# Cross-attention over eight batches: query chunks 4 to 7 of batches 0 and 1 by seven products of sums, and the softmax of seven quads divided after the value products

## The chip, the core and the metric

The program runs on one core of a Trainium2 chip. The metric is the device time of one execution, in microseconds; the median of three executions stands for a kernel. The core has five engines that run their own instruction streams in order: TensorE (PE in the profile, with its weight loads as PEld), VectorE (DVE), ScalarE (ACT), GpSimd (POOL) and SyncE (SP), which only issues transfers here. They wait for each other by semaphores. All data are 32-bit floats.

## The reference

One layer of cross-attention: layer norm of x, a query projection, attention of 32 heads of 32 columns over 256 context rows (which are keys and values at once), an output projection, and the residual.

```python
x = (hidden - mu) * rsqrt(var + 1e-5) * ln_gamma + ln_beta      # (8, 256, 1024)
Q = split_heads(x @ Wq.T)                                       # 32 heads of 32
scores = einsum('bhsd,bhtd->bhst', Q, K) * 32 ** -0.5           # K = V = context, (8, 256, 1024)
probs = softmax(where(mask, scores, -inf))
attn = einsum('bhst,bhtd->bhsd', probs, V)
return hidden + attn.reshape(B, S, 1024) @ Wout.T
```

## The kernel before

Work is cut into 64 **quads**. Quad n is batch n // 8 and query chunk n % 8: 128 columns of Q, which are four heads (0 to 3). For a quad, PE makes eight score products (`scores`, tiles `sc_n_j`, one PSUM bank a head, and there are four such banks in all, so the scores of quad n+1 overwrite those of quad n). VectorE adds the mask and takes the row's extreme (`exps`, the rows named CUSTOM_DVE_ANT_0 in the profile and ISA in an order, two for each head), ScalarE takes the exponential and sums it (tile `den`), VectorE inverts the sum (`normalize`, RECIPROCAL to `rden`), GpSimd or ScalarE multiplies the 128x256 tiles `e` by it, VectorE transposes them in blocks (`blocks`, STREAM_TRANSPOSE to `pT`), four transfers of SyncE swap blocks between partitions, with ScalarE's copies `pc` between, and PE multiplies with the values (`values`, tiles `pv`, 64 products a quad written as 32 in each of two halves). ScalarE copies the result to `at` (`copy_at`), in which the columns of a head stand on partitions.

A **query chunk** is `make_q`: eight products of 128x128 weights `wq` with `xnT`, eight for each of eight chunks and each batch. Batches 2 to 7 already go in pairs with seven products of sums instead of eight (`sum_x`, `sum_wq`, `query_product`, `copy_product`): the sums of weights replace the weights in `wq` and `ring`. Batches 0 and 1 go chunk by chunk. Chunks 0 to 2 of batch 0 stand ahead of the loop over quads, the others are spread over n = 0 to 9. Batch 0 carries one more column (257): the product of the weights with beta, which is the bias that batch 1 and later add in `copy_q`. Batch 0 is scaled by gamma in `copy_x0`; later batches have gamma folded into the weights (`fold`, eight sums 128x1024 on GpSimd).

The output projection of batch b runs in the eight quads after it (`product_steps`, tiles `po`), also by seven products of sums (`sum_wo`, `sum_at`).

What sets the order: all calls are recorded (`Recorded`) and issued by a table written out by number (`ORDER`), which fixes the order on each engine. The semaphores follow from it.

Names that the change and the prediction touch: `copy_x0`, `copy_x1`, `make_q`, `copy_q`, `fold`, `exps`, `normalize`, `copy_at`, the tiles `gs`, `qlo`, `ring`, `wo` (sums of output weights, empty early on), and `rp` (four tiles of 128x512, for residual rows, unused until the residuals of batch 0 are loaded).

## Time and profile before

| | us |
|---|---|
| median of three runs (lowest, highest) | 562.45 (561.54, 562.81) |
| the profiled execution's own time | 562.03 |
| span of its profile, first to last instruction | 560.2 |
| busy: PE, DVE, ACT, POOL | 553.7, 461.4, 441.1, 402.9 |
| chain that ended last: share of PE | 96% |

The span is what the prediction works on; 1.8 us lie around it. A row of the groups reads: line, engine, operation, tile written and tiles read, shape, count, then busy time, the mean length of one, and the idle time of that engine just before, with what ended it. Every instruction has the same line number, 371, since one recording helper issues them all, so tiles and not lines tell them apart. PE's records: one 128x128x256 product of the program is two records in the trace, so that a chunk of eight products shows as x16.

### The profile page before, as it was taken

The numbers are of one execution on the slowest core, as the hardware profiler recorded it, in microseconds if no ns is written. First come the engines' busy times: TensorE is split into PE (matmuls) and PEld (weight loads), VectorE is DVE, ScalarE is ACT, GpSimd is POOL, SyncE is SP. The second block draws the span as 40 slices with busy tenths as digits, with TensorE's granted clock in tenths as the row PEclk, the third lists the DMA queues.
The fourth block names the chain that finished last, engine by engine and source line by source line (L and its number), as shares of the span: only waits on it lengthen the run. The fifth ranks groups of instructions, "written<-read, shape, count | busy, mean of one in ns | idle before, by whom it ended". The sixth has DMA issues, their size and how long they took to land.

```text
span 560.2 us, 18699 instructions
## 1 busy us (share of the span) xinstructions
PE 553.7 (99%) x6586; PEld 371.3 (66%) x6586; DVE 461.4 (82%) x1709; ACT 441.1 (79%) x1475; POOL 402.9 (72%) x633
## 2 busy tenths in 40 slices
PE   7999999999999999999999999999999999999997
PEld 6778786676666675667675677566666666645544
DVE  5899889988788999878989889876786888888725
ACT  3599999889886797879777779878879768989930
POOL 1479989999789856678969676478773778467581
PEclk9999999999999999999999999999999999999999
DMA  8977777867587676789666867878657476765342
GB/s 298 346 228 236 201 207 207 245 163 198 177 262 250 182 204 183 204 234 273 164 183 209 221 174 209 240 206 226 152 158 212 112 218 187 221 197 135 95 115 112
DMA packets 46477, 112.64 MB, mean 201 GB/s; under 512 B 9008, under 2 KB 9776, under 8 KB 46384
## 3 DMA queue, kind: packets, MB, share of 16 engines
q1 hardware_dynamic: 40384, 91.52, 57.5%
q0 software_dynamic: 5712, 19.93, 11.5%
q8 instruction: 52, 0.85, 0.7%
q14 instruction: 41, 0.34, 0.2%
q10 hardware_dynamic: 288, 0.01, 0.0%
HBM read 58.99 MB, written 12.58 MB: 128 GB/s over the span
## 4 chain that ended last, share of the span: by engine, by line
PE 96%; DMA 2%; DVE 1%; issue 0%; ACT 0%
PE pq_P L371 26%; PE po_S L371 20%; PE sc L371 12%; PE pv L371 11%; PE po_A L371 11%; PE pq L371 10%; PE po_end L371 3%; PE po_last L371 1%; DMA x<-in_x_dram 1%; DMA k<-in_kv_dram 1%; PE px L371 1%; DMA gam<-in_gamma_dram 1%; PE po_end_s L371 0%; DVE pT L371 0%; DVE mb L371 0%; DVE e L371 0%
## 5 line engine op out<-in xcount | busy, mean ns | idle before, releaser
L371 ACT ACTIVATE e<-e,mn 128x256 f32<-128x256 f32 x512 | 256.0, 502 | 61.0 <-DVE mn L371 56.8
L371 POOL TENSOR_SCALAR e<-e,rden 128x256 f32<-128x256 f32 x408 | 191.4, 480 | 113.9 <-DVE rden L371 107.0
L371 DVE STREAM_TRANSPOSE pT<-e 128x512 f32<-128x512 f32 x256 | 177.3, 701 | 33.2 <-POOL e L371 24.4
L371 DVE CUSTOM_DVE_ANT_0 e<-sc,mb 128x256 f32<-128x256 f32 x512 | 192.4, 411 | 8.6 <-PE sc L371 4.0
L371 PE MATMUL pq_P<-xnT,wq 128*128 128x256 f32 x544 | 133.2, 383 | 0.1
L371 PEld LDWEIGHTS pq_P<-xnT,wq 128*128 128x128 f32 x544 | 101.5, 190 | 44.9 <-issue 29.6
L371 ACT ACTIVATION_READ_ACCUMULATOR e<-e,mn 128x1 f32 x512 | 97.2, 190 | 0.0
L371 ACT COPY pc<-pT 128x512 f32<-128x512 f32 x128 | 76.2, 611 | 11.1 <-DVE pT L371 8.4
L371 PE MATMUL po_S<-wo,at 128*128 128x512 f32 x152 | 74.0, 598 | 0.0
L371 DVE RECIPROCAL rden<-den 128x2 f32<-128x2 f32 x256 | 36.5, 151 | 32.2 <-ACT e L371 31.4
L371 PE MATMUL pq<-xnT,wq 128*128 128x256 f32 (+3 forms) x272 | 60.0, 372 | 1.3 <-DVE xnT L371 0.8
L371 PE MATMUL po_A<-wo,at 128*128 128x512 f32 x128 | 60.2, 600 | 0.0
L371 PE MATMUL pv<-pT,v_all 64*32 64x128 f32 x3584 | 59.4, 273 | 0.0
L371 PEld LDWEIGHTS pv<-pT,v_all 64*32 64x32 f32 x3584 | 51.3, 105 | 11.3 <-issue 5.7
L371 PEld LDWEIGHTS pq<-xnT,wq 128*128 128x128 f32 x272 | 48.0, 190 | 10.2 <-issue 2.8
L371 ACT ACTIVATE e<-e,rden 128x256 f32<-128x256 f32 x104 | 49.6, 501 | 3.3 <-DVE rden L371 3.1
L371 PE MATMUL po_S<-wo,s 128*128 128x512 f32 x104 | 51.0, 600 | 0.0
L371 PE MATMUL sc<-k,qa 32*128 32x256 f32 x640 | 47.4, 401 | 0.0
L371 PEld LDWEIGHTS sc<-k,qa 32*128 32x128 f32 x640 | 30.0, 184 | 18.9 <-issue 10.6
L371 DVE DVE_READ_ACCUMULATOR2_ANT mn<- 128x1 f32 x512 | 42.5, 83 | 0.0
L371 PEld LDWEIGHTS po_S<-wo,at 128*128 128x128 f32 x152 | 28.1, 190 | 19.4 <-issue 16.4
L371 PEld LDWEIGHTS po_A<-wo,at 128*128 128x128 f32 x128 | 23.5, 190 | 24.5 <-issue 22.5
(97 smaller groups left out, 603.6 us busy)
## 6 DMA issues: line engine op xcount, KB each, us to landing
pT<-pT SPq DMA_DIRECT2D x128, 128.0 KB, 3.2
pT<-pc SPq DMA_DIRECT2D x128, 128.0 KB, 3.7
v_all<-in_kv_dram POOLq DMA_DIRECT2D x17, 512.0 KB, 5.0
k<-in_kv_dram SPq DMA_DIRECT2D x30, 256.0 KB, 3.8
r<-in_x_dram SPq DMA_DIRECT2D x26, 256.0 KB, 4.3
xnT<-xe SPq DMA_DIRECT2D x92, 64.0 KB, 3.5
out_dram<-r POOLq DMA_DIRECT2D x18, 256.0 KB, 3.5
wq<-in_wq_dram SPq DMA_DIRECT2D x8, 512.0 KB, 8.5
```

What stands on the lines that cost most here:

```text
L371: getattr(getattr(self.nc, other.get(i, engine)), name)(*a, **k)
```

## The change

Three things, and a new order table.

Chunks 4 to 7 of batches 0 and 1 (a 512-column half of Q, 512 rows in two batches) are made by seven products of sums, of eight 128x128x256 matmuls each (`head_product`), where `make_q` took eight such groups. Four sums of weights (`head_sum_w`, in two halves each, 128x512) go to parts of `wo` that are empty early on; four sums of inputs (`head_sum_x`, in two halves each) go to `ring`, into batch 0's `xnT` and to `wo`. The products' results are copied or added by `head_copy`. Chunks 0 to 3 are made as before.

So that sums of both batches fit together, gamma is applied to batch 1's rows too (`copy_x1`, now eight ScalarE instructions with scale and bias, 128x256, where four plain copies of 128x512 stood), the score's scale is applied to gamma and beta beforehand, and `copy_q` is a plain copy. `fold` of the weights comes later.

Quads 1 to 7 are no longer divided before the value products. Their 28 reciprocals on VectorE and 56 multiplications of 128x256 (40 on GpSimd, 16 on ScalarE) go. In their place `turn_dens` makes, for each quad, one reciprocal of the 128x8 sums, one block transpose of 128x32, a transfer to DRAM and one back that spreads it over the partitions (128x256, into tiles of `rp`), and `copy_at` is followed by one GpSimd product of 128x256.

```diff
+    def head_sum_w(to, o, engine=nc.gpsimd):
+        a, b = {"T1": ("B12", "B11"), "T2": ("B22", "T1"), "T3": ("T2", "B11"), "T4": ("B21", "T2")}[to]
+        engine.tensor_tensor(H_T[to][:, o], H_T[a][:, o], H_T[b][:, o], ALU.subtract)
+
+    def head_sum_x(to, part, engine=nc.gpsimd):
+        a, b, op = {
+            "S1": ("A21", "A22", ALU.add), "S2": ("S1", "A11", ALU.subtract),
+            "S4": ("A12", "S2", ALU.subtract), "S3": ("A22", "S2", ALU.subtract),
+        }[to]
+        to, a, b = (H_X[of]()[:, ts(part, 2), :S] for of in (to, a, b))
+        engine.tensor_tensor(to, a, b, op)
+
+    def head_product(name):
...
+        if begins:
+            h_po[0] = ps_q.tile([P, 512], F32, tag="pq", name=f"ph_{name}_0")
+            h_po[1] = ps_o.tile([P, 512], F32, tag="po", name=f"ph_{name}_1")
+        wide = x_.shape[2]
+        for o in range(2):
+            for c in range(NK):
+                nc.tensor.matmul(
+                    h_po[o][:, :wide], w[:, o, c], x_[:, c], start=begins and c == 0, stop=c == NK - 1,
+                    skip_group_check=True,
+                )
+
+    def head_copy(name, o):
+        po = h_po[o]
+        if name in ("P1", "P2", "P5"):
+            to = {"P1": h_u[:, o], "P2": qa[:, H + o], "P5": h_v[:, o]}[name]
+            nc.scalar.copy(to, po[:, : S + 1])
+        elif name == "P6":
+            nc.vector.tensor_tensor(h_u[:, o, :S], po[:, :S], h_u[:, o, :S], ALU.add)
+            nc.gpsimd.tensor_tensor(h_v[:, o], h_v[:, o], h_u[:, o], ALU.add)
+        elif name == "P3":
+            nc.vector.tensor_tensor(qa[:, H + 2 + o], po[:, : S + 1], h_v[:, o], ALU.add)
...
+    HEAD_Q = {1: ("P1",), 2: ("P2",), 3: ("P5",), 4: ("P6", "P3"), 8: ("P7", "P4")}
+    HEAD_W = {0: ("T1", "T2"), 1: ("T3", "T4")}
+    HEAD_X = {1: ("S1",), 2: ("S2",), 3: ("S4", "S3")}
...
+    def turn_dens(n):
+        away = dram.tile([K, NA * K], F32, tag=f"dens_{n}", name=f"dens_{n}")
+        nc.vector.reciprocal(dens_of[n][:, : 2 * NH], dens_of[n][:, : 2 * NH])
+        nc.vector.transpose(turned[n], dens_of[n])
+        nc.sync.dma_start(
+            away.rearrange("c (a k) -> a c k", a=NA),
+            turned[n],
+        )
+        nc.sync.dma_start(
+            factors[n],
+            away[: 2 * NH].rearrange("(j s) q -> j (s q)", j=NH).unsqueeze(1).to_broadcast([NH, HD, T]),
+        )
...
+            if n in DEFER:
+                if j == 1:
+                    turn_dens(n)
+                return
...
+        if NQ * b + NK * k + c in DEFER:
+            at = ats[b, k][:, c].rearrange("p s a k -> p (s a k)")
+            nc.gpsimd.tensor_tensor(at, at, factors[NQ * b + NK * k + c], ALU.mult)
...
- 'foldat': [1, 1, 3, 3, 4, 5, 6, 7],
+ 'foldat': [5, 6, 7, 8, 3, 3, 4, 4],
...
-0-38 40-41 39 44 42 47 43 49-50 45 54-59 61 60 62-75 79-81 77 84-86 93 76 78 83 87-90 94-95 91-92 96-109
+32-33 35 34 36-38 43 40 39 42 41 44 51 50 46 45 54-55 0-19 56 58 57 59-60 64 84-85 61-63 65-71 20-24 72-74
```

What the new table does is seen in the engines' rows. First PE, between the scores of quad 5 and those of quad 6. Before, after the value products of quad 1, it reads (`pq_n` is the n-th query chunk, 8 and up are batch 1's):

```order
L371 MATMUL pq_7_262<-xnT_0_132,wq_120 128x257 x3
L371 MATMUL pq_8_286<-xnT_1_180,wq_120 128x256 x3
L371 MATMUL pq_9_291<-xnT_1_180,wq_120 128x256 x6
L371 MATMUL pq_8_286<-xnT_1_180,wq_120 128x256 x3
L371 MATMUL sc_6_0_312<-k_6_268,qa_119 128x256
```

and now, from the last row of quad 5's scores on (`ph_P6_0` and `ph_P6_1` are the two halves of the product P6):

```order
L374 MATMUL ph_P6_0_266<-xnT_0_132,wo_126 128x256
L374 MATMUL ph_P6_1_267<-xnT_0_132,wo_126 128x256
L374 MATMUL ph_P6_0_266<-xnT_0_132,wo_126 128x256
L374 MATMUL ph_P6_1_267<-xnT_0_132,wo_126 128x256 x2
L374 MATMUL ph_P3_0_268<-xnT_0_132,wq_120 128x257
L374 MATMUL ph_P6_1_267<-xnT_0_132,wo_126 128x256
L374 MATMUL ph_P3_0_268<-xnT_0_132,wq_120 128x257
L374 MATMUL ph_P3_1_269<-xnT_0_132,wq_120 128x257
L374 MATMUL ph_P3_0_268<-xnT_0_132,wq_120 128x257 x2
L374 MATMUL ph_P3_1_269<-xnT_0_132,wq_120 128x257 x2
L374 MATMUL pq_8_288<-xnT_1_184,wq_120 128x256 x2
```

Products of sums of batch 0 stand where two chunks of batch 1 stood, and the first of batch 1 comes only at the end; one bank takes P6_0, P3_0 and then chunk 8.

Second, VectorE in the same place, where quad 5's mask-adds end and its transposes begin. Before:

```order
L371 ISA e_5_2_300,mn_5_2_301<-sc_5_2_289,mb_0_142 128x256
L371 ISA mn_5_2_301 128x1
L371 STREAM_TRANSPOSE xe_2_308<-x_2_214 128x32x32
L371 RECIPROCAL rden_5_1_307<-den_5_1_299 128x2
L371 STREAM_TRANSPOSE pT_5_292<-e_5_0_294 128x8x64
L371 ISA e_6_0_321,mn_6_0_322<-sc_6_0_312,mb_0_142 128x256
L371 ISA mn_6_0_322 128x1
L371 RECIPROCAL rden_5_3_310<-den_5_3_306 128x2
```

and now:

```order
L374 ISA e_5_3_278,mn_5_3_279<-sc_5_3_265,mb_0_146 128x256
L374 ISA mn_5_3_279 128x1
L374 RECIPROCAL qlo_121<-qlo_121 128x8
L374 STREAM_TRANSPOSE pT_5_270<-e_5_0_272 128x8x64
L374 TENSOR_TENSOR qa_119<-ph_P3_1_269,ring_105 128x257
L374 STREAM_TRANSPOSE pT_5_270<-e_5_1_274 128x8x64
L374 STREAM_TRANSPOSE pT_5_270<-e_5_2_276 128x8x64
L374 ISA e_6_1_295,mn_6_1_296<-sc_6_1_283,mb_0_146 128x256
```

The reciprocals of single heads are gone from between, one for a whole quad is there, and an addition out of PSUM (P3's second half) has come in.

Third, GpSimd from quad 0's last multiplication on. Before:

```order
L371 TENSOR_SCALAR e_0_3_161<-e_0_3_161,rden_0_3_174 128x256 x2
L371 TENSOR_SCALAR e_1_1_188<-e_1_1_188,rden_1_1_198 128x256 x2
L371 TENSOR_SCALAR e_1_0_185<-e_1_0_185,rden_1_0_194 128x256 x2
L371 TENSOR_SCALAR e_1_2_191<-e_1_2_191,rden_1_2_199 128x256 x2
L371 TENSOR_SCALAR e_1_3_195<-e_1_3_195,rden_1_3_200 128x256 x2
L371 TENSOR_TENSOR wq_120<-wq_120,gs_118 128x1024
```

and now (`wo<-wq` are the sums of weights, `ring<-xnT` and `xnT<-ring` the first sums of inputs, `x_2` the layer norm of batch 2):

```order
L374 TENSOR_SCALAR e_0_3_165<-e_0_3_165,rden_0_3_178 128x256 x2
L374 TENSOR_TENSOR wo_126<-wq_120 128x512
L374 TENSOR_TENSOR wo_126<-wq_120,wo_126 128x512 x2
L374 TENSOR_TENSOR wo_126<-wo_126,wq_120 128x512
L374 TENSOR_TENSOR wo_126<-wq_120 128x512
L374 TENSOR_TENSOR wo_126<-wq_120,wo_126 128x512 x2
L374 TENSOR_TENSOR wo_126<-wo_126,wq_120 128x512
L374 TENSOR_TENSOR rstd_2_235<-ve_2_0_237,mhalf_110 128x1
L374 TENSOR_TENSOR ring_105<-xnT_1_184 128x2x256 x2
L374 TENSOR_SCALAR x_2_211<-x_2_211,mv_2_234,rstd_2_235 128x1024
L374 TENSOR_TENSOR xnT_0_132<-ring_105,xnT_0_132 128x2x256
```

Eight sums of 128x512 and then sums of inputs stand where quads 1 and later were multiplied.

443 lines of the change are left out of this document (245 added, 198 removed).

## The prediction

> **What bounds the kernel now.** First the page: its busy line, PE's slices and the chain that ended last.
>
> ```profile
> span 560.2 us, 18699 instructions
> PE 553.7 (99%) x6586; PEld 371.3 (66%) x6586; DVE 461.4 (82%) x1709; ACT 441.1 (79%) x1475; POOL 402.9 (72%) x633
> PE   7999999999999999999999999999999999999997
> PE 96%; DMA 2%; DVE 1%; issue 0%; ACT 0%
> ```
>
> TensorE is busy in every slice but the first and the last, and 96% of the chain is its own work. A busy row can hide waits, so second the table of who waited for whom, PE alone, which is complete with these five rows:
>
> ```profile
> PE busy L371 <- POOL ring masks.py:199: 1.4, 1, 1.4
> PE pq L371 <- DVE xnT L371: 0.8, 1, 0.8
> PE pq L371 <- ACT xnT L371: 0.5, 1, 0.5
> PE px L371 <- DVE x L371: 0.4, 1, 0.4
> PE sc L371 <- issue: 0.3, 1, 0.3
> ```
>
> All 3.4 us of it lie in the first 13 us. Third, pieces of the chain in order of time (start, length, what, count), for the price of a piece of PE's work:
>
> ```profile
> 59.61 2.04 PE pv L371 x119
> 104.44 1.09 PE pv L371 x64
> 105.52 2.77 PE po_S L371 x6
> 115.83 2.58 PE po_S L371 x6
> 118.40 3.45 PE pq_P L371 x16
> ```
>
> A chunk of eight query products (x16) takes 3.45 us, 0.43 a product; an output product takes 0.86 (2.58 for three). The same three cost 0.2 more where a run of full-width products begins after scores or values (2.77). The values of two quads together take 2.04, of one 1.09. So after the head the time is the sum of PE's pieces, and what is taken off PE comes off the end, as long as nobody else becomes late.
>
> The Trainium skill's page "Perfetto Trace Analysis" (Identifying the Most-Contended Engine) says that matmul busy time is no good measure of how near TensorE is to its roofline, and that the busy share of the weight loads is, which is 66% here; by that rule there would be air in PE and fewer products need not show. This trace speaks against it: the pieces above follow each other without a wait, so I take PE as the bound and keep the rule as a rival.
>
> Who else is close? Busy time in stretches, from the first scores of quad 1 (22.9 us) to those of quad 11 (96.0), and two stretches within:
>
> ```profile
> core 0: us, PE busy (x) PEld busy (x) DVE busy (x) ACT busy (x) POOL busy (x), PEclk, DMA share, GB/s
> 22.90:96.00 73.10, 73.10 (x909) 56.97 (x908) 67.05 (x260) 68.67 (x226) 65.28 (x95) 1.00 0.75 214
> 28.80:55.70 26.90, 26.90 (x286) 21.77 (x283) 26.11 (x105) 26.37 (x89) 23.92 (x34) 1.00 0.80 237
> 55.70:88.20 32.50, 32.50 (x429) 26.29 (x427) 28.50 (x111) 31.19 (x104) 29.82 (x42) 1.00 0.75 203
> ```
>
> All engines stand at 89 to 94% here, which is where the change is made; this stretch decides.
>
> **TensorE.** Chunks 4 to 7 of two batches took 64 products and take 56. Eight times 0.43 is **3.45 us** off. By the order, runs of full-width products go from 70 to 71 (+0.2) and values from 27 pairs and 10 single quads to 29 and 6 (29 x 2.04 + 6 x 1.09 against 27 x 2.04 + 10 x 1.09: -0.3). Net -3.5. Width 257 instead of 256 falls on 56 products in both.
>
> **The other three in quads 1 to 10.** Prices:
>
> ```profile
> L371 DVE CUSTOM_DVE_ANT_0 e<-sc,mb 128x256 f32<-128x256 f32 x512 | 192.4, 411 | 8.6 <-PE sc L371 4.0 <-DVE rden L371 0.4
> L371 DVE RECIPROCAL rden<-den 128x2 f32<-128x2 f32 x256 | 36.5, 151 | 32.2 <-ACT e L371 31.4
> L371 DVE STREAM_TRANSPOSE pT<-e 128x512 f32<-128x512 f32 x256 | 177.3, 701 | 33.2 <-POOL e L371 24.4 <-ACT e L371 5.5 <-DMA pT<-pT 1.1
> L371 POOL TENSOR_SCALAR e<-e,rden 128x256 f32<-128x256 f32 x408 | 191.4, 480 | 113.9 <-DVE rden L371 107.0 <-ACT e L371 3.8 <-DMA xnT<-xe 0.6
> L371 POOL TENSOR_TENSOR wo<-wo 128x512 f32<-128x512 f32 x15 | 19.1, 1276 | 0.0
> L371 POOL TENSOR_TENSOR s<-at,at 128x256 f32<-128x256 f32 x2 | 1.5, 735 | 4.4 <-ACT at L371 4.4
> L371 POOL TENSOR_TENSOR wq<-wq,gs 128x1024 f32<-128x1024 f32 x8 | 15.1, 1898 | 0.0
> L371 ACT ACTIVATE e<-e,rden 128x256 f32<-128x256 f32 x104 | 49.6, 501 | 3.3 <-DVE rden L371 3.1
> L371 ACT ACTIVATE qa<-pq,qa 128x256 f32<-128x256 f32 x8 | 3.6, 466 | 0.7 <-PE pq L371 0.6
> L371 ACT COPY xnT<-px 128x512 f32<-128x512 f32 x4 | 2.2, 581 | 0.0
> ```
>
> PE's own work from quad 1's scores to quad 11's shrinks from 73.1 to **69.0 us**: eight products (3.45), one output product that the new order puts behind the stretch (0.86), one more run (+0.2).
>
> VectorE has, by the order, the same 80 mask-adds, 38 big transposes and layer norm work there. Of reciprocals there are 38 before and 18 after: 20 x 0.143 (36.5/256) = -2.9. Seven transposes of 128x32 come in, not in this trace: bounds are a reciprocal's 0.15 and the big transpose's 0.70; 0.2, near the small end for a sixteenth of the elements: +1.4. Eight additions of 128x256 out of PSUM, priced as the mask-add, which also reads PSUM: 8 x 0.41 = +3.3 (at most 0.68 by twice the columns, not taken). Sum 67.05 + 1.8 = **68.9 of 69.0 us**. That is full. But busy sums count overlaps:
>
> ```profile
> 54.63 0.42 DVE L371 CUSTOM_DVE_ANT_0 e<-sc,mb 128x256 f32<-128x256 f32 x1
> 54.98 0.42 DVE L371 CUSTOM_DVE_ANT_0 e<-sc,mb 128x256 f32<-128x256 f32 x1
> ```
>
> Back to back, mask-adds start 0.35 apart, against 0.376 each in the sum (192.4/512); for 80 that is 2.5 us of air, so that it needs 66.4 if packed. In its best stretch (28.80 to 55.70) VectorE was busy 97.1%. At that share the work takes 68.4 (packed) to 71.0 us (not): 0 to 2.0 us longer than PE's. Since quad n+1's scores need the four banks that VectorE's last mask-add of quad n frees, PE waits for what is missing.
>
> GpSimd loses 38 multiplications (0.469 each, -17.8), one fold (-1.9), one other sum (-1.3) and two transfers; it gains 16 sums of 128x512 (+20.3) and six products or sums of 128x256 (+4.4): about +2.5, so 67.8 of 69.0. It too is nearly full, though its sums stand well ahead of their readers in the order: the last S2 has some 3 us to spare before P6. ScalarE loses 16 multiplications (-7.6), has 12 query copies for 14 (-0.9), and eight scaled copies for four plain ones (8 x 0.46 - 2.2 = +1.5): 62 of 69, and is no longer the tightest.
>
> For lateness of VectorE, with a full GpSimd beside it, I take **+1.3 us**, inside 0 to 2.0 but above its middle, and keep up to 4 for the range. Behind a late VectorE addition stands PE itself: the one bank takes P6_0, P3_0 and chunk 8 in turn, with two products (0.86 us) between an end and the next begin.
>
> **The new transfers.** Each quad's sums go out and back in two steps. Nearest rows:
>
> ```profile
> pT<-pT SPq DMA_DIRECT2D x128, 128.0 KB, 3.2
> xnT<-xe SPq DMA_DIRECT2D x92, 64.0 KB, 3.5
> ```
>
> Two in a row are 7 us; the factor is read after the value products three quads later, some 20 us. Hidden: 0. On SyncE they stand among the block swaps, and a wait of one holds those behind it; swaps have their first reader over 10 us after the last transpose by the order, and without this cover each us would be PE's.
>
> **The head.**
>
> ```profile
> 0.72 0.20 POOL masks.py:197 MEMSET ring<- 128x128 f32 x1 [0.29 <-POOLq L1639]
> 1.35 5.14 PE L371 MATMUL busy<-ring 128*128 128x128 f32 x32 [1.35 <-POOL ring masks.py:199]
> 6.00 0.81 DVE L371 TENSOR_SCALAR x<-x,mv,rstd 128x1024 f32<-128x1024 f32 x1 [0.77 <-POOL rstd L371]
> 7.11 1.29 DVE L371 BATCH_NORM_STATS2 st<-x 128x6 f32<-128x512 f32 x2 [0.29 <-DMA x<-in_x_dram]
> 12.48 0.71 PE L371 MATMUL sc<-k,qa 32*128 32x256 f32 x8
> ```
>
> VectorE's order puts half of the second statistics (0.65) into the 0.77 us that it waited, so the second half of x is normalized earlier; scores could begin up to 0.8 earlier than 12.48. The next weights and the ScalarE copies are as they were, so I take -0.3 (0 to -0.8). The 128x448 fill put on GpSimd ahead of the first fillers costs three to four times 0.20, in idle time.
>
> **Sum.** -3.5 + 1.3 - 0.3 = -2.5 on the profiled execution's 562.03, so 559.5; that execution lies 0.4 under the median 562.45, which gives 559.9; I say **559.8**.
>
> **Rivals.**
> - *Nobody is late* (0.12): VectorE packs as the 0.35 spacing allows; -3.5 - 0.5: 558.3.
> - *VectorE takes the gain* (0.14, no change): at a share of 95% its 68.9 takes 72.5, 3.5 more than PE's 69.0; time 562. For it: 68.9 of 69.0. Against: 97.1% was reached over 27 us.
> - *VectorE is the bound at its poorer share* (0.09, slower): between 55.70 and 88.20 it was busy 28.50 of 32.50, 87.7%; so 68.9 would take 78.6, 9.6 late: 568. It decides from a share below 94.6% (72.8, 3.8 late) on. Against: in that stretch ScalarE was at 31.19 of 32.50 and held it, and ScalarE loses 6 us.
> - *PE had air* (0.03, no change): the removed products were hidden, as the weight loads' 66% could suggest; 562.
> - *The clock falls in the head* (0.02, no change): the fillers now end after 20, then come in pieces between waits of 1 to 2 us. In the 5.14 us of 32 fillers the early ones run at half the rate of the later. If PE fell back for 3.4 us, half of that is lost: +1.7, 561.5. The Trainium skill ("TensorE: Matmul & The Clock Gate", The HAM clock gate) has the clock halved after an idle window of about 3.4 us; no gap here is that long, so by it nothing is lost.
>
> **How the numbers follow.** The forecast has 0.60 (558.6 to 561.2). About 0.2%, 1.1 us, is what a measurement of this kernel can tell from no change. Faster: 0.60 + 0.12 = 0.72; within: 0.14 + 0.03 + 0.02 = 0.19; slower 0.09. The range 558.2 to 562.6 leaves out the slower case and the fringe of the best.
>
> **What would show it.** PE's records of query products fall by 16, and a chunk's price stays 3.45. Between quad 1's and quad 11's scores: about 70.3 us, VectorE at 97% or more, ScalarE under 90%. PE waits newly listed for VectorE (mask-adds, `ph_P` banks), 1 to 2 us in all, inside the first 100 us. First scores at 12.2. Wrong would be: a stretch of 72 us or more (VectorE or GpSimd the bound), PE waits for `factors` or `at`, or new waits behind quad 14, where the new order has no cause of its own to stall.

## The result and the profile after

| | before | after |
|---|---|---|
| median of nine runs each (lowest, highest) | 562.22 (561.52, 562.81) | 565.67 (564.77, 569.71) |
| the profiled execution's own time, its span | 562.03, 560.2 | 569.71, 567.9 |

The changed kernel takes 1.0076 times as long (95% interval 1.0051 to 1.0100): slower, where the prediction said faster. The profiled execution of after is the longest of its nine; the same kernel profiled once more (e0 below) took 565.73. The runs of after scatter over 5 us, those of before over 1.3. Ratios, here and below, are of means, without the one run that was in a slower state (e4's 572.26).

The page of after, its busy line, PE's slices and the chain that ended last:

```profile
span 567.9 us, 18645 instructions
PE 556.1 (98%) x6570; PEld 371.1 (65%) x6570; DVE 464.3 (82%) x1703; ACT 436.4 (77%) x1461; POOL 410.4 (72%) x621
PE   6999999998999999999999999999999999999997
PE 77%; DMA 7%; DVE 7%; ACT 4%; issue 2%; SPq 1%; POOL 1%; DVEq 0%; ACTq 0%
```

PE has 16 records fewer, as the change intended, and is yet busy 2.4 us longer, and only 77% of the chain is its work instead of 96%: transfers, VectorE and ScalarE have come onto the path. The table of PE's waits (us in total, times, longest), before five rows and all in the head, now has waits for transfers, and the values (`pv`) among those who wait:

```profile
PE pv L374 <- issue: 2.1, 1, 2.1
PE px L374 <- DVE x L374: 1.9, 1, 1.9
PE busy L374 <- POOL ring masks.py:199: 1.8, 1, 1.8
PE pq L374 <- ACT xnT L374: 0.8, 1, 0.8
PE pv L374 <- DMA pT<-pc: 0.6, 1, 0.6
PE sc L374 <- DMA k<-in_kv_dram: 0.5, 1, 0.5
```

Not every wait shows as idle time in these rows. Where PE waits within a run of scores or values, the records of that run are drawn out instead and count as busy: in e3 below, the scores of quad 9 take 4.1 us where a quad's scores take 1.07, and only 1.28 us of it are listed as waits.

To see how much each stretch loses, PE's stream was cut into its runs of scores, values and full-width products. The time from the first record of a run to the first record of the next, less the undisturbed price of that run (1.07 for a quad's scores, 2.04 and 1.09 for values of two quads and of one, 0.215 for each record of a 256-column product, and so on), is what PE lost there. The prices add up to 540.7 us before and 537.2 in every version of after. The losses, by the quads whose scores begin the stretch:

| us lost in quads | before | after | e0 | e3 | e8 | e9 | e11 | e12 | e17 |
|---|---|---|---|---|---|---|---|---|---|
| head and 0 | 4.21 | 5.98 | 6.61 | 6.28 | 4.67 | 5.50 | 6.85 | 4.65 | 4.78 |
| 4–7 | 0.29 | 1.70 | 1.71 | 1.71 | 1.69 | 1.31 | 1.69 | 1.70 | 1.69 |
| 8–10 | 0.05 | 1.03 | 1.06 | 4.71 | 0.11 | 0.0 | 0.02 | 0.90 | 1.22 |
| 11–13 | 0.01 | 1.97 | 1.16 | 0.01 | 2.63 | 0.02 | 0.06 | 0.97 | 0.86 |
| 14–19 | 0.23 | 4.33 | 1.57 | 1.02 | 1.39 | 0.76 | 0.88 | 1.69 | 0.91 |
| 40–49 | 0.28 | 1.38 | 0.20 | 0.55 | 0.29 | 0.13 | 2.88 | 6.49 | 0.84 |
| all others | 1.83 | 1.22 | 1.34 | 1.10 | 0.74 | 0.92 | 1.39 | 0.91 | 0.94 |
| sum | 6.90 | 17.61 | 13.65 | 15.38 | 11.52 | 8.60 | 13.77 | 17.31 | 11.24 |

Prices and losses of after add 7.2 us to those of before, of the span's 7.7. Another 0.4 is PE's start: the first of its fillers (the products `busy` at the start, row 3 of the waits) begins at 1.76 instead of 1.35, behind the 128x448 fill on GpSimd. The table shows a cost in five places, one after the other.

**The head.** From after's timeline (start, length, engine, operation, and in brackets the idle time before and what ended it):

```profile
6.60 0.69 DVE L374 BATCH_NORM_STATS2 st<-x 128x6 f32<-128x512 f32 x1 [1.27 <-DMA x<-in_x_dram]
7.21 0.80 DVE L374 TENSOR_SCALAR x<-x,mv,rstd 128x1024 f32<-128x1024 f32 x1
8.80 1.28 ACT L374 ACT_TABLE_LOAD   x1 [8.80 <-PE px L374]
10.10 1.50 ACT L374 ACTIVATE xnT<-px,bet,gs 128x128 f32<-128x128 f32 x4
14.66 0.71 PE L374 MATMUL sc<-k,qa 32*128 32x256 f32 x8
```

The half statistics that were to fill VectorE's 0.77 us now stand ahead of the normalization, and they wait for the second half of x until 6.60; the normalization starts at 7.21 (before 6.00). And ScalarE loads its table at 8.80, between the transposed x and its first scaled copy. In the trace of before it stood early:

```profile
4.37 1.28 ACT L371 ACT_TABLE_LOAD   x1 [4.37 <-DMA bet<-in_beta_dram]
```

The table load follows the wait of the first activation. That waited for beta before, and now, since gamma and beta come scaled from other tiles, it waits for PE.

**Quads 1 to 10.** The stretch of the prediction, from the scores of quad 1 to those of quad 11, in the view by windows:

```profile
core 0: us, PE busy (x) PEld busy (x) DVE busy (x) ACT busy (x) POOL busy (x), PEclk, DMA share, GB/s
25.07:96.18 71.11, 70.81 (x890) 53.15 (x889) 67.63 (x252) 64.02 (x214) 65.96 (x68) 1.00 0.73 204
```

It took 71.1 us (before 73.1, forecast 70.3), with VectorE at 95% (67.63 of 71.11) and ScalarE at 90%.

**The swaps.** Median time from issue to landing in after's table of transfers (before 3.2 and 3.7), and a piece of after's chain of waits (start, length), at the swap of quad 9's blocks:

```profile
pT<-pT SPq DMA_DIRECT2D x128, 128.0 KB, 3.8
pT<-pc SPq DMA_DIRECT2D x128, 128.0 KB, 4.0
...
95.31 7.17 DMA pT<-pT
103.10 2.70 DMA pT<-pc
```

A swap goes in two halves, forward (`pT<-pT`) and, after ScalarE's copy, the way back (`pT<-pc`). A forward half that usually takes 3 to 4 us takes 7.2 here. It was issued behind four fetches of the sums (91.10 to 93.96) and quad 8's way back, and PE then waits for the values of quad 9.

**A wait and a slow clock.** At 131.73, in quads 11 to 19, PE waited 2.08 us for the values (the row `pv <- issue` above), and then ran at half rate. Two windows of after (columns as above):

```profile
128.87:132.28 3.41, 1.33 (x50) 0.94 (x44) 1.62 (x4) 0.55 (x3) 1.42 (x4) 1.00 0.41 87
132.28:135.70 3.42, 3.42 (x116) 2.95 (x96) 2.08 (x5) 3.05 (x9) 3.20 (x4) 0.50 0.48 121
```

PEclk, the granted clock, is 0.50 for 3.4 us, so some 1.7 us more are lost. e0 has neither; its clock falls once too, but in the head (7.92 to 11.33).

### The profile page after: what moved, and what is told of

It reads as the page before. It is cut to its first block, busy times and chain, and to the rows that moved or that the text cites. A ratio compares the mean times of both kernels' runs of the same rounds, so it can differ in the third digit from the quotient of the medians.

```text
span 567.9 us, 18645 instructions
## 1 busy us (share of the span) xinstructions
PE 556.1 (98%) x6570; PEld 371.1 (65%) x6570; DVE 464.3 (82%) x1703; ACT 436.4 (77%) x1461; POOL 410.4 (72%) x621
## 4 chain that ended last, share of the span: by engine, by line
PE 77%; DMA 7%; DVE 7%; ACT 4%; issue 2%; SPq 1%; POOL 1%; DVEq 0%; ACTq 0%
PE pq_P L374 23%; PE po_S L374 17%; PE pv L374 10%; PE sc L374 10%; PE po_A L374 10%; DMA pT<-pT 4%; PE po_end L374 3%; DVE e L374 3%; DVE pT L374 2%; ACT e L374 2%; PE pq L374 2%; DMA pT<-pc 2%; PE ph_P L374 1%; PE po_last L374 1%; SPq L374 1%
## 5 line engine op out<-in xcount | busy, mean ns | idle before, releaser
L374 POOL TENSOR_SCALAR e<-e,rden 128x256 f32<-128x256 f32 x368 | 172.2, 480 | 120.6 <-DVE rden L374 118.5
L374 PE MATMUL pv<-pT,v_all 64*32 64x128 f32 x3584 | 61.5, 277 | 3.0 <-issue 2.1
L374 PEld LDWEIGHTS pv<-pT,v_all 64*32 64x32 f32 x3584 | 53.0, 107 | 14.6 <-issue 9.0
L374 DVE RECIPROCAL rden<-den 128x2 f32<-128x2 f32 x228 | 32.7, 152 | 29.1 <-ACT e L374 27.8
L374 PE MATMUL sc<-k,qa 32*128 32x256 f32 x640 | 48.6, 402 | 0.6 <-DMA k<-in_kv_dram 0.5
L374 ACT ACTIVATE e<-e,rden 128x256 f32<-128x256 f32 x88 | 41.5, 502 | 7.0 <-DVE rden L374 6.5
L374 ACT COPY at<-pv 128x128 f32<-128x128 f32 x128 | 30.1, 253 | 17.5 <-PE pv L374 17.5
L374 PE MATMUL pq<-xnT,wq 128*128 128x256 f32 (+3 forms) x144 | 31.7, 363 | 1.1 <-ACT xnT L374 0.8
```

The lines of the kernel that those rows point to most:

```text
L374: getattr(getattr(self.nc, other.get(i, engine)), name)(*a, **k)
```

## The experiments

Each row of the table is one kernel; the losses above are read from the one profiled execution of each.

| run | median (lowest, highest), runs | ratio to before (95%) |
|---|---|---|
| e0 unaltered | 566.72 (565.73, 568.65), 4 | 1.0081 (1.0058, 1.0104) |
| e1 table load early | 568.40 (565.96, 570.17), 4 | 1.0096 (1.0061, 1.0131) |
| e2 normalization first | 565.36 (565.22, 567.98), 5 | 1.0057 (1.0037, 1.0077) |
| e3 no transfers of sums | 568.62 (567.88, 569.39), 4 | 1.0103 (1.0086, 1.0120) |
| e4 e1 and e2 | 566.06 (563.45, 572.26), 6 | 1.0054 (1.0025, 1.0084) |
| e5 mask bias on GpSimd | 577.65 (576.24, 579.21), 4 | 1.0271 (1.0244, 1.0298) |
| e6 fetches behind swaps | 568.05 (566.18, 569.93), 4 | 1.0102 (1.0071, 1.0133) |
| e7 e4, e5 and e6 | 578.00 (576.89, 578.49), 4 | 1.0276 (1.0261, 1.0292) |
| e8 e4, mask bias on ScalarE | 567.51 (563.90, 571.46), 7 | 1.0090 (1.0058, 1.0122) |
| e9 e8 without the turn | 562.41 (560.82, 564.22), 12 | 0.9998 (0.9983, 1.0012) |
| e10 e8, fetches behind swaps | 567.19 (563.82, 568.58), 6 | 1.0094 (1.0081, 1.0107) |
| e11 e8, fetches of 4 partitions | 564.02 (562.86, 569.09), 9 | 1.0042 (1.0021, 1.0063) |
| e12 e8, turn on ScalarE's queue | 564.35 (562.41, 569.41), 9 | 1.0043 (1.0021, 1.0064) |
| e13 e8, a load of x later | 567.20 (565.28, 569.65), 6 | 1.0067 (1.0046, 1.0087) |
| e14 e12, e13, fill on VectorE | 564.59 (562.06, 569.08), 12 | 1.0032 (1.0008, 1.0055) |
| e15 e8, each fetch in four | 569.58 (568.98, 572.04), 5 | 1.0125 (1.0107, 1.0143) |
| e16 e15, fill on VectorE | 571.24 (568.65, 573.01), 5 | 1.0161 (1.0134, 1.0187) |
| e17 e14, 32 fillers first | 563.58 (561.75, 567.38), 12 | 1.0026 (1.0009, 1.0044) |

### e0: the changed kernel once more

No edit; its profile is the one to which the others are compared.

> The changed kernel unaltered, to have a second profile of it on the chip of the next three runs: its nine runs lay between 564.8 and 566.3 us but for two at 569.4 and 569.7, and the profile on record is one of those two. If the waits of the value products between 103 and 135 us (5.2 us there, one of 2.1) belong to the kernel, they are here again and the time is 565 to 570; if they are a chance of that one execution, TensorE's excess over its sum between 100 and 140 us falls from 6.5 to about 2 us and the time is 565.

Its profile (565.73) has the head, quads 4 to 7, 8 to 10 and 11 to 13 of after, but neither the 2.08-us wait nor the clock's fall behind it, and nothing in quads 40 to 49. So the losses up to quad 13 belong to the kernel, and the large ones later to some executions.

### e1, e2, e4: the head

In e1 a small activation stands right behind the load of beta on ScalarE:

```diff
+                if i == 33:
+                    self.nc.scalar.activation(*self.warm, AF.Identity)
```

> One activation of 128x2 more on ScalarE right behind its two loads, so that the table load no longer stands behind the wait for the first transposes of x (in the changed kernel it runs from 8.80 to 10.08 us, before from 4.37 to 5.65). If that load is on the path to the first scores, they come 0.8 to 1.3 us before 14.66 and the whole is 0.8 to 1.3 us shorter. Rival: VectorE alone sets the first scores (its normalization starts at 7.21 where it was 6.00); then the time stays within 0.3 us.

In e2 the last steps of the first half's layer norm go ahead of the second half's statistics:

```diff
-32-33 35 34 36-38 43 40 39 42 41 44 51 50 46 45 54-55 0-19 56 58 57 59-60 64 84-85 61-63 65-71 20-24 72-74
+32-33 35 34 36-38 43 40 39 42 41 44 51 50 46 45 54-55 0-19 56 58 57 59-60 84-85 61-62 64 63 65-71 20-24 72-74
```

> VectorE normalizes the first half of batch 0 ahead of the statistics of its second half, as before the change. If these statistics, which wait for their load until 6.60 us, hold the normalization up, it starts at 6.0 in place of 7.2 us, and first scores and end come 0.8 to 1.2 us earlier. Rival: ScalarE's table load behind the transposes keeps the path; then first scores still move with the transposes, by 1.2, since the load waits for them: if instead only the loads from DRAM set them, nothing moves.

e4 has both.

> Both edits of the head together: ScalarE's table load ahead of its wait, and the first normalization ahead of the second half's statistics. If these two make the head's lateness, first scores come at 12.3 to 13.1 us in place of 14.5 to 15.3, and the time falls by 1.8 to 2.4 us. Rival: the loads, which the new order brings in another sequence, set it; then first scores stay at 13.5 or later.

The first scores begin at 14.66 and 15.29 in after and e0, 13.90 in e1, 14.46 in e2 and 13.35 in e4 (before 12.48). e4's lies between the 12.3 to 13.1 expected and its rival's 13.5. From e4's timeline:

```profile
1.64 1.28 ACT L376 ACT_TABLE_LOAD   x1 [1.64 <-PEq L1753]
...
6.11 0.81 DVE L374 TENSOR_SCALAR x<-x,mv,rstd 128x1024 f32<-128x1024 f32 x1 [0.76 <-POOL rstd L374]
...
13.35 0.71 PE L374 MATMUL sc<-k,qa 32*128 32x256 f32 x8
```

Both causes are shown in the trace: the table is loaded at 1.64, the normalization starts at 6.11, and about 1.3 to 1.9 us of the head come back. The medians can't show it: these kernels scatter by 3 to 9 us from run to run, e1's profile lost 4.27 us in quads 40 to 49, and the intervals of e2 and e4 overlap with that of e0.

### e3, e5, e6, e7: transfers and the mask bias, confounded

e3 leaves out the 14 transfers of the sums; four plain loads of 256 KB early on fill the factors instead, so that the later products take other numbers.

```diff
-        nc.sync.dma_start(
-            away.rearrange("c (a k) -> a c k", a=NA),
-            turned[n],
-        )
-        nc.sync.dma_start(
-            factors[n],
-            away[: 2 * NH].rearrange("(j s) q -> j (s q)", j=NH).unsqueeze(1).to_broadcast([NH, HD, T]),
-        )
+        nc.skip.dma_start()
+        if DEFER.index(n) % 2 == 0:
+            nc.sync.dma_start(factors_in[DEFER.index(n) // 2], x[0, :P, :512])
+        else:
+            nc.skip.dma_start()
```

> The 14 transfers of the reciprocal sums are left out; the four tiles of factors are filled by four plain loads instead, so the attention of quads 1 to 7 is multiplied by the wrong numbers. If the 14 issues and their waits on SyncE push the block swaps of quads 10 to 14 back (TensorE waits for them and for loads behind them at 103 to 135 us), the excess of TensorE between 100 and 140 us goes down to 1 to 2 us and the time falls by 2 to 4 us. Rival: the lateness comes from the order of the other transfers, or from VectorE and GpSimd; then the time stays within 0.7 us.

The loss in quads 11 to 13 was gone (0.01), as the theory of the transfers asks, but 4.71 us stood in quads 8 to 10, some 1.7 of them at a halved clock (below). From the timelines: first VectorE and GpSimd in e0, at the mask bias of batch 1 (`mb`, 128x256; before it took 0.27):

```profile
74.59 1.91 POOL L374 TENSOR_TENSOR wq<-wq,gs 128x1024 f32<-128x1024 f32 x1
75.00 1.65 DVE L374 TENSOR_SCALAR mb<-mk 128x256 f32<-128x256 uint8 x1
...
77.38 0.73 POOL L374 TENSOR_TENSOR at<-at,factors 128x256 f32<-128x256 f32 x1 [0.43 <-DMA factors<-dens]
```

and the same in e3:

```profile
74.27 1.91 POOL L375 TENSOR_TENSOR wq<-wq,gs 128x1024 f32<-128x1024 f32 x1
74.68 3.95 DVE L375 TENSOR_SCALAR mb<-mk 128x256 f32<-128x256 uint8 x1
76.12 0.21 POOL L375 TENSOR_TENSOR gam<-qa 128x4 f32<-128x4 f32 x1
76.30 0.26 POOL L375 TENSOR_SCALAR shift<-mv,rstd 128x1 f32<-128x1 f32 x1
76.53 0.72 POOL L375 TENSOR_TENSOR at<-at,factors 128x256 f32<-128x256 f32 x1
77.22 1.26 POOL L375 TENSOR_TENSOR ring<-wq 128x512 f32<-128x512 f32 x1
```

VectorE's instruction ends 0.15 us after one of GpSimd's: in e0 after the fold of weights (76.65 against 76.50), in e3 only after four more of GpSimd's (78.63 against 78.48). In before this instruction met no fold; `fold` is what the new table moved beside it. The Trainium skill, "SBUF — State Buffer" (🔬 SBUF: two separate sides), says that VectorE, where its instruction is in a two-port mode or has two inputs in SBUF, shares a port pair with GpSimd as an exclusive lock, whose loser stands still for the other's whole instruction. Whether this instruction is of that kind, no run shows. The two ends agree with such a lock, though by it VectorE would have gone on in e3 after the first instruction, and it stood through five. What decides between the two, the records don't show.

e5 moves that mask bias to GpSimd.

```diff
-OTHER = {}
+OTHER = {779: 'gpsimd'}
```

> The mask bias of batch 1 (128x256, at 75.0 us on VectorE) is made by GpSimd. In the profile of the changed kernel repeated, it takes 1.65 us where the first one takes 0.24, and ends 0.15 us after GpSimd's 128x1024 product that runs beside it; without the transfers it took 3.95 and ended 0.15 us after the third GpSimd product in a row. If VectorE stands still there because GpSimd is at work, and this is what makes the scores of quad 9 late (0.6 us of waits) and the product behind them (0.3), these go to 0.1 and the time falls by 0.5 to 1.0 us. Rival: VectorE is late there anyway by its load; then the scores of quad 9 keep 0.4 us or more of waits.

e6 moves three fetches on SyncE behind the swaps of quads 8 and 9 (one line of the table ahead, one behind):

```diff
-915 497 981 1005 573 760 699 920 919 1017-1024 1089-1091 1224 986 985 682 979 978 993 989 988 991 983 990 1015
+915 497 981 1005 920 919 1017-1024 1089-1091 1224 986 985 682 979 978 993 989 988 991 983 990 1015 1092
...
+1097-1098 872 1025-1088 1095-1096 995 997 996 1014 1107 1105-1106 994 998 1001-1002 1004 1003 573 760 699 1108
```

> Three of the seven fetches of factors, which stand in a row on SyncE ahead of the block swaps of quads 8 and 9, are moved behind them. In the changed kernel repeated, a swap of quad 9 takes 7.5 us to land behind their 128-KB broadcasts (packets of 1 KB), SyncE waits 5.6 us for it and is behind until 128 us. If it is these fetches, the swap lands in 3 to 4.5 us, the values of quads 8 and 9 (wait at 104 to 107: 1.1) and of the next pair (129 to 131: 0.7) come without waits, and the time falls by 1.5 to 2 us. Rival: the number of transfers on SyncE, not their place; then the waits stay, and SyncE issues without pause until 125 us or later all the same.

e7 has the edits of e4, e5 and e6 together.

> All four edits of the runs e4 to e6 in one kernel. If the three causes are separate, their gains add: 1.8 to 2.4, 0.5 to 1.0 and 1.5 to 2.0 off 565.7 to 566.7, so 560.5 to 562.5, that is equal to before or up to 2 us under it. Rival: they hide each other, and it stays at 563.5 or above.

e5 made a wait of its own: GpSimd, which runs ahead of VectorE, stood 11.49 us until it could write the one `mb` tile, and 13.15 us were lost in quads 8 to 10 (13.55 in e7). e6 met the mask bias at 3.95 us again, as e3 did. None of the three told the theories apart; they led to e8.

### e8 and e9: the mask bias away, then the turn of the sums

e8 is e4 with that mask bias on ScalarE:

```diff
+        if b in (1,):
+            nc.scalar.activation(mbs[b], mks.pop(b), AF.Copy, bias=MASKED, scale=-MASKED)
+        else:
```

> The head as in e4, and the mask bias of batch 1 made by ScalarE, which stands idle for 2 us there waiting for VectorE. If VectorE's standstill beside GpSimd (1.8 us in e4, up to 3.95 when GpSimd has no pause) is the cause of the waits of the scores of quad 9, these go from 0.8 to under 0.2 us, and the time falls from e4's 563.5 (its least) to 562.3 to 562.9, with less scatter than e4's 563.5 to 572.3. Rival: VectorE is late there by its load alone; then 0.4 us or more of these waits stay.

e9 is e8 without the reciprocal, the transpose and the transfers of `turn_dens`, with e3's plain loads in their place.

```diff
-        nc.vector.reciprocal(dens_of[n][:, : 2 * NH], dens_of[n][:, : 2 * NH])
-        nc.vector.transpose(turned[n], dens_of[n])
...
+        nc.skip.reciprocal()
+        nc.skip.transpose()
```

> e8 without the reciprocals, the transposes and the transfers of the sums of quads 1 to 7 (14 VectorE instructions of 0.2 us, 14 issues on SyncE; four plain loads fill the factors, so quads 1 to 7 are multiplied by the wrong numbers). If VectorE's load makes the waits of quads 4 to 7 (1.7 us: scores of quad 4, the one bank of the products), they fall to 0.3 to 1.0; if the new transfers make those of the values at 103 to 131 us, these fall from 1.2 to 1.9 to under 0.3: then the time is 558.5 to 560.5. Rival for the second: the place of other transfers in the new order; then those waits stay as in e8.

In e8 the mask bias takes 0.40 us on ScalarE and the loss in quads 8 to 10 falls from 1.06 (e0) and 1.21 (e4) to 0.11. But quads 11 to 13 rise from e4's 0.74 to 2.63: PE comes earlier and meets the same late swap. The median, expected at 562.3 to 562.9, did not come down (567.51, e4's 566.06). From e8's chain of waits:

```profile
93.65 7.09 DMA pT<-pT
...
101.36 2.72 DMA pT<-pc
...
104.22 1.25 PE pv L374 x63
```

The forward swap of quad 9, issued at 93.65 behind three fetches, lands after 7.09 us, the way back follows, and the values wait for it. In e9 the loss in quads 11 to 13 is 0.02 and PE's list of waits has only the three rows of the head:

```profile
PE busy L375 <- POOL ring masks.py:199: 1.8, 1, 1.8
PE px L375 <- DVE x L375: 0.7, 1, 0.7
PE pq L375 <- DVE xnT L375: 0.3, 1, 0.3
```

By medians e9 is 5.1 us under e8 (567.51 and 562.41; the intervals of the ratios lie apart), and its runs scatter over 3.4 us where e8's scatter over 7.6. The two profiles differ by less: 2.9 us of losses (11.52 and 8.60), of which 2.6 lie in quads 11 to 13; e8's is its fastest run. A part of the rest is the clock. The mean granted clock of e8's three faster runs (563.90 to 566.55) is 1.000, that of its four slower ones (567.51 to 571.46) 0.996 or 0.997, as in the run of after with 3.4 us at half rate; in e9 it is 0.998 or more. Where those four runs waited is not shown. Once the head and the mask bias are mended, the turn of the sums is the largest cost that a run shows. Without it the kernel is as fast as before (0.9998), not faster, and short of the 558.5 to 560.5 expected: its profile still loses 1.3 us more than before in the head, 1.0 in quads 4 to 7 and 0.5 in 14 to 19, and starts 0.4 later.

### e10, e11, e12, e15, e16: what of the turn costs

e10 is e6's edit on e8.

> e8 with the three fetches of factors behind the block swaps of quads 8 and 9 as in e6, which then told nothing, since VectorE stood still for 3.95 us ahead of it. If the place of the three fetches makes the waits of the values at 103 to 131 us, they fall from 1.2 to 1.9 to under 0.5 us and the time is 560.5 to 561.8. Rival: the product on GpSimd that needs these factors comes late instead and holds the sums behind it, or the number of transfers matters and not the place; then no gain, 562 to 563.

The loss stayed, 2.47 in quads 11 to 13. SyncE's issues in e10's timeline:

```profile
92.25 1.14 SPq L374 DMA_DIRECT2D pT<-pT  x2
93.44 1.74 SPq L374 DMA_DIRECT2D factors<-dens  x3
...
95.80 1.33 SPq L374 DMA_DIRECT2D pT<-pc  x2
```

The way back is now issued 3.55 us behind the forward swap (95.80), but its two transfers stand behind the fetches, and the second, issued at 96.57, takes 7.08 us.

e11 is e8 with fetches that write 4 partitions instead of 128 (4 KB instead of 128), so that most factors are ones; all 14 issues stay.

```diff
-            factors[n],
-            away[: 2 * NH].rearrange("(j s) q -> j (s q)", j=NH).unsqueeze(1).to_broadcast([NH, HD, T]),
+            factors[n][:NH],
+            away[: 2 * NH].rearrange("(j s) q -> j (s q)", j=NH),
```

> e8 with all 14 transfers of the sums issued at their places, but each fetch of factors brings 4 partitions in place of 128 (4 KB for 128 KB; the tiles are filled with ones once, so quads 1 to 7 are multiplied by wrong numbers in all but 4 partitions). If the packets of these broadcasts (128 of 1 KB each) make the block swaps land late, the waits of the values at 100 to 131 us fall from e8's 3.2 to under 0.5 us, the scatter with them, and the time comes near e9's 562.4 (560.8 to 564.2). If the issues on SyncE and their own waits do it, the waits stay above 2 us and the time at 566 to 568.

Quads 11 to 13 lose 0.06. In its timeline the fetches stand at the same place, and the way back of quad 9's swap follows the forward one by 3.6 us instead of 7.1:

```profile
93.50 1.00 SPq L374 DMA_DIRECT2D factors<-dens  x3
...
95.80 2.48 SPq L374 DMA_DIRECT2D pT<-pT  x2
...
99.43 1.15 SPq L374 DMA_DIRECT2D pT<-pc  x2
```

So the 128-KB fetches delay the swaps behind them, and not the issues, the waits on SyncE or the small transfers out; whether by their bytes, the number of their packets or their shape, this run doesn't tell. Its median (564.02) lies 3.5 under e8's, though here the intervals of the ratios overlap; its profile had a slow head (first scores 15.53) and 2.88 us in quads 40 to 49.

e12 puts the 14 transfers on ScalarE's queue, at later places in its order.

```diff
-        nc.sync.dma_start(
+        nc.scalar.dma_start(
```

> e8 with the 14 transfers issued on ScalarE's queue, each placed behind an instruction that starts 0.5 us after its data are there by e8's trace. If it is SyncE's order of issue, the waits of the values at 100 to 131 us fall below 0.5 us, and the time is 559.5 to 562 unless ScalarE, which had 7 us left between the scores of quads 1 and 11 and gets 6 to 7 us of issues, becomes late (then scores and the one bank of the products wait more than e8's 1.7 us in quads 4 to 10). If it is the traffic of the broadcasts on the 16 DMA engines, 1.5 us or more of these waits stay.

Quads 11 to 13 lose 0.97 instead of 2.63, with 0.90 in quads 8 to 10 again: a part of it (in e14 and e17, with the transfers on the same queue, quads 11 to 13 lose 0.05 and 0.86). Its profile is its longest run, with 6.49 us in quads 40 to 49; a clock at half rate for 6.8 us makes some 3.4 of them (below).

e15 splits each fetch of e8 by its four heads; e16 adds e14's fill (below).

```diff
+                if engine == "four":
+                    to, of, hd, nh, t = a
+                    for j in range(nh):
+                        self.nc.sync.dma_start(to[ts(j, hd)], of[j : j + 1].to_broadcast([hd, t]))
```

> e8 with each fetch of factors (4 rows of 1 KB, each copied to 32 partitions, in one transfer whose outermost dimension is 4) split into four transfers of 32 partitions each, so that the outermost dimension is 32. In e10, between 96 and 98 us, such packets alone run at some 85 GB/s while the share of the 16 DMA engines is 0.27, about 4 of 16, and the block swap issued behind them lands 7 us later: if one fetch occupies only four engines, and the swaps wait there behind it, then in four pieces it is through in a third of the time, and a swap of quad 9 is followed by its second half after 3.5 to 4.5 us in place of 7.1; the waits of the values at 100 to 131 us fall from e8's 3.2 to 0.5 to 1.0 us and the time to 562.5 to 564.5 by the median. Rival: 21 more issues of 0.5 us on SyncE make it as late as before; then it stays at 566 to 568.

> e15 with the 128x448 fill on VectorE in place of GpSimd, where it stood ahead of the first fillers: TensorE starts at 1.35 in place of 1.76 us. If TensorE's clock and the first transposes hang on that start, 0 to 0.4 us less than e15; since the first transposes wait for x in any case, the same within the scatter is as likely.

From e15's timeline:

```profile
95.66 6.75 SPq L377 DMA_DIRECT2D factors<-dens  x12
...
103.70 1.18 SPq L379 DMA_DIRECT2D pT<-pT  x2
...
106.00 1.18 SPq L379 DMA_DIRECT2D pT<-pc  x2
```

Twelve issues took 6.75 us of SyncE, and the swap that waited behind them then needed only 2.3. The lateness went from the transfer to its issue (8.81 and 6.76 us lost in quads 11 to 13 of e15 and e16, with half rates of 6.8 and 3.4 us in them), so this doesn't tell whether a fetch of another shape would be harmless.

### e13, e14, e17: the later quads, and the best of all parts

e13 moves a 512-KB load of x (call 6158, at 405 us) to 449, since quads 40 to 49 lose time in some executions.

```diff
-4993 4988 4982 4980 4990-4991 4693 4628 4876 4989 6158 4689-4690 4815 4818 4814 4871 4930-4961 4992 4983 4994
...
+5211-5218 5157-5158 5208 5219 5832 5081 5076 5080 6158 6009 5020 5186 5190 5189 5082 5185 5195-5196 5176-5178
```

> e8 with one load moved: the new order brings the last batch's 512-KB residual at 404.9 us, right behind two 512-KB loads of kept sums and between the block swaps of quads 44 to 46, while before it stood at 460.8. In the profiles of e1, e2, e11 and e12 TensorE loses 2.9 to 6.5 us between the scores of quads 40 and 49, in e0, e4, e8 and e10 0.2 to 0.4. If that load in that place makes the difference between the executions, the scatter shrinks from e8's 563.9 to 571.5 to some 3 us, and the median falls from 567.5 to 563 to 565. Rival: the scatter comes from the head or from the swaps at 100 to 131 us; then spread and median stay.

Its profile lost 2.77 us there without that load. This theory fell.

e14 is e12 with that load later and the 128x448 fill on VectorE, so that PE's fillers start at 1.35 as before.

```diff
-OTHER = {}
+OTHER = {54: 'vector'}
```

> e12 (fetches by ScalarE) with that load moved too, and the 128x448 fill ahead of the first fillers put on VectorE, which is idle there (TensorE's first filler then starts at 1.35 as before and not at 1.75). By the profile of e12, 6.5 us of waits between quads 40 and 49 go and 0.4 in the head; its least time 562.4 would fall to some 561.5 and the median to 561 to 563, so equal to before within 0.2 per cent or a little under it. Rival: ScalarE's issues make other waits in quads 8 to 19 (3.6 us in e12), and it stays above 563.

e17 is e14 with all 32 fillers at the start, as in before.

```diff
-32-33 35 34 36-38 43 40 39 42 41 44 51 50 46 45 54-55 0-19 56 58 57 59-60 84-85 61-62 64 63 65-71 20-24 72-74
+32-33 35 34 36-38 43 40 39 42 41 44 51 50 46 45 54-55 0-31 56 58 57 59-60 84-85 61-62 64 63 65-74 76-78 80
```

> e14 with all 32 fillers at the start again, as before the change, in place of 20 and twelve spread between the waits of the head. In the profiles, TensorE's clock is at full rate from 4.3 us on before, and in the kernels with 20 fillers from 4.5 to 6.8 us in some executions and only from 10.5 to 11.3 us in others (e0, e2, e9, e11, e13); their first scores are at 14.2 to 15.5 us, also with the mended head, where those of e4, e8, e10 and e12 are at 13.3 to 13.5. If the clock is what the spread fillers cost, it is full by 5 us here, first scores come at 12.9 to 13.4 us (e14: 13.9), and the median is 0.5 to 1.5 us under e14's 564.6, the scatter smaller. Rival: the loads of x make the difference between these executions; then first scores stay at 13.4 to 14.5 and the median within 0.4 us.

In e14 the clock came to full only at 10.1 us and the first scores at 13.94; in e17 at 6.7 and at 13.05, the earliest of all versions of after. e17's 1.0026 (1.0009 to 1.0044) is the best that kept the whole computation: still above before. No version was faster than before.

## Why the prediction was wrong, point by point

- **PE's content, -3.5: right.** 16 records fewer, and the prices fall from 540.7 to 537.2. Where nobody is late, PE's pieces take the same time in after as in before, so the removed records were not hidden in air; nothing here speaks for the rival by the weight loads' share.
- **VectorE's lateness, +1.3: near in size, by a mechanism only partly named.** Quads 1 to 10 lose 3.06 us in after against 0.95 before, so 2.1 more; with the mask bias off VectorE (e8) 2.13, so 1.2 more. That part is the one forecast. In quads 4 to 7 of e8 VectorE is busy for 29.33 of 30.39 us, and after's timeline has quad 4's scores drawn out (quad 5's are beside them), the rest of them starting at 44.28, when the mask-add of 43.79 is through:

```profile
43.51 1.89 PE L374 MATMUL sc<-k,qa 32*128 32x256 f32 x16
43.79 0.42 DVE L374 CUSTOM_DVE_ANT_0 e<-sc,mb 128x256 f32<-128x256 f32 x1
50.28 1.15 PE L374 MATMUL sc<-k,qa 32*128 32x256 f32 x16
```

As this is no idle time, the 1 to 2 us of waits that were to be newly listed for VectorE are not in the list; behind the head it has one of 0.2. The air of 80 mask-adds, put at 2.5 us, is 2.1 by the prediction's own spacing (0.026 each), which leaves its range of 0 to 2.0 as it is. The other 0.9 is the mask bias beside `fold`, which I had not seen: I summed busy times of VectorE and GpSimd apart, as if an instruction's length did not depend on what runs beside it. Over the whole stretch VectorE stood at 95%, not at the 97% that I asked for, and the slower rival (the poorer share, a stretch of 78.6) did not come: it took 71.1. That the time came near that rival's 568 is chance.
- **The new transfers, "Hidden: 0": the step that failed.** I asked whether the factor comes in time for its own reader, and it nearly does (GpSimd waited 0.43 us for one in e0, in the row shown with e3). I did name that SyncE holds the swaps behind a wait, and took ten microseconds of cover for enough. What failed is neither: with fetches of 128 KB under way the next swap lands in 7.1 us instead of 3 to 4 (e8 against e11), and the swap and its way back then come after PE. That is 1.2 to 2.6 us in quads 11 to 13 of the profiles (e0, after, e8). By medians e8 against e9 puts 5.1 us on the whole turn, e8 against e11 3.5 on the large fetches, the latter with intervals that overlap.
- **The head, -0.3: the second step that failed, wrong in sign.** The first scores come 2.2 us later in after and 2.8 in e0; in e0's profile this is the largest miss of all. I gave VectorE's idle 0.77 us to the second half's statistics without asking when their data land; the row at 7.11 in the prediction, idle 0.29 for the load of x, had the answer. And I held ScalarE's copies to be "as they were", though their operands, and with them the place of the table load, had changed (e1, e2, e4: 1.3 to 1.9 us back). The fill ahead of the first fillers, held to lie in idle time, moved PE's start by 0.4; e16, which takes it away again, was no faster than e15.
- **The clock.** The rival in the head had a part: with 20 fillers the clock came to stay at full rate only at 10.1 to 13.0 us in eight profiles, instead of at 4.3 in before and 6.7 in e17 with all 32, worth about a microsecond (e14 against e17: 13.94 and 13.05). Behind the head I had said nothing of it, and eight profiles show a fall there, below.
- **"New waits behind quad 14, where the new order has no cause of its own": wrong as an exclusion.** Quads 14 to 19 lose more than before in every version of after: 0.3 to 2.0 us in the experiments, 4.1 in after with its fall of the clock. In quads 40 to 49 some executions lose 2.8 to 6.5 us (e1, e2, e11, e12, e13) and others 0.1 to 1.4, and the runs of after scatter over 5 us. In e12 half of it is the clock's fall; what made PE wait there first stays open, and e13 ruled out one load.

Put together on e0, against before: content -3.5, head +2.4, quads 4 to 7 +1.4, 8 to 10 +1.0, 11 to 13 +1.2, 14 to 19 +1.3, the rest -0.6, and PE's later start +0.4: +3.6 of the 3.7 between the spans of the two profiled executions. The head makes 2.8 of it where -0.3 was forecast, quads 4 to 10 make 2.4 where 1.3 was, and quads 11 to 19, where nothing was, 2.5; only about 1.2 of that last part, in quads 11 to 13, is traced to the fetches.

## What to carry to other kernels

Price a new transfer by what it does to those behind it, not by whether its own reader can wait: here seven fetches off the path cost, by medians, about as much (3.5 us) as the products that they helped to save. Idle time may be filled only by an instruction whose data are there; the trace says in brackets when they land. And where four engines stand at 90% and more, a gain on the one that is the bound brings it earlier to everything that was just in time, so that mending one wait (the mask bias, e8) can return as another (the swap, 0.74 to 2.63).

## What the runs showed of the hardware

The granted clock fell also behind waits shorter than the time for which it stayed down: in after PE waited 2.08 us, and the half rate lasted 3.4 us, some 1.7 us of work. Behind the head eight profiles show such a fall: after, e3, e13 and e16 one of 3.4 us, e12 and e15 one of 6.8, e5 one of 10.2, and e7 two, of 10.2 and 3.4. e3's two windows and the fall of e12 (columns as above):

```profile
81.85:85.26 3.41, 2.75 (x17) 1.81 (x18) 2.92 (x16) 3.41 (x13) 2.75 (x7) 1.00 0.36 82
85.26:88.67 3.41, 3.41 (x10) 2.70 (x9) 2.39 (x9) 3.41 (x8) 3.41 (x5) 0.50 0.56 146
...
417.83:424.66 6.83, 6.83 (x21) 4.42 (x21) 5.04 (x15) 5.21 (x19) 6.63 (x11) 0.50 0.53 137
```

In e3 PE counts as busy for 2.75 of the 3.41 us before the fall, but these are drawn-out scores:

```profile
81.91 1.10 PE L375 MATMUL sc<-k,qa 32*128 32x256 f32 x4 [0.68 <-DVE mn L375]
83.61 1.12 PE L375 MATMUL sc<-k,qa 32*128 32x256 f32 x10 [0.60 <-DVE mn L375]
```

At undisturbed prices the window holds 14 score records (0.067 each) and three of a 256-column product (0.215), some 1.6 us of work, 46%. Reckoned in this way (an estimate), and in windows of 3.41 us counted from each profile's changes of the clock, the falls before the program's end all stand behind windows with less than half of such work: 32% in after, 46% in e3, 47% in e12, 44% at the second fall of e7. Under a third the clock fell each time, nine of nine; but e10's window with the 1.35-us wait for the values of quad 9, at 48%, and e8's at 46% had no fall behind them. The Trainium skill, "TensorE: Matmul & The Clock Gate" (What's actually happening), has the clock go down after an idle window of about 3.4 us; the length of the step agrees with the measured 3.41, but these windows were not idle. Between a third and a half, these runs don't settle the condition.

A standstill of VectorE beside GpSimd has no fixed price: one instruction of 128x256 took 0.27 us in before, 1.65 in after and e0, and 3.95 in e3 and e6, in the same place of the program. Before knew it too: the same instruction of a later batch took 1.92 us there, at 274.85, and ended 0.16 us after a sum on GpSimd.
